# A decoder kernel: three places for the exponentials, squares moved right behind the maxima, and queries normed within the first step

## The chip, the cores and the metric

The kernel runs as one program on one core of a Trainium2 chip. The core has five engines with a queue of instructions each: PE multiplies matrices and transposes by a product with an identity matrix, DVE does elementwise work, reductions and transposes of 32x32 squares, ACT does activations and copies, POOL does elementwise work, and SP does nothing here but issue transfers. The metric is the device time of one execution in microseconds (us). The kernel before takes 907.77 us, the median of three runs (907.56 to 908.26).

## The reference

Eight sequences of 128 tokens with 512 features pass through two decoder layers. Each layer has an attention, a cross attention and a feed-forward block, each followed by a residual sum and a layer norm:

```python
x = _layernorm(x + _L0_attn_ref(x, ...))                 # causal, 32 heads of 16
x = _layernorm(x + _L0_xattn_ref(x, ctx_4096, ctx_4096)) # autocorrelation
x = _layernorm(x + _L0_ffn_ref(x, ...))                  # 28 experts of rank 8, two chosen
x = _layernorm(x + _L1_attn_ref(x, ...))                 # the block of the change
x = _layernorm(x + _L1_xattn_ref(x, ctx_4096, ...))      # 16 heads of 96, 4 key heads
x = _layernorm(x + _L1_ffn_ref(x, ...))                  # 8 adapters of rank 16
```

The change touches the second layer's causal attention alone:

```python
qkv = jnp.clip(jnp.einsum('bsd,ed->bse', hidden_states, Wqkv), -8.0, 8.0)
q, k, v = jnp.split(qkv, [512, 1024], axis=-1)
q = _layer_norm(q, q_ln_w, q_ln_b)       # mean and variance over all 512 features
k = _layer_norm(k, k_ln_w, k_ln_b)
# q, k, v are cut into 32 heads of 16
scores = jnp.einsum('bqhd,bkhd->bhqk', q, k) * 16 ** -0.5
scores = scores + slopes[None, :, None, None] * rel[None, None]   # distance of the tokens
scores = jnp.where(causal[None, None], scores, -1e30)
probs = jax.nn.softmax(scores, axis=-1)
out = jnp.einsum('bhqk,bkhd->bqhd', probs, v).reshape(B, S, 512)
return jnp.einsum('bsd,ed->bse', out, Wout)
```

## The kernel before

All in all the kernel goes through the six blocks one after the other, all in float32. The second causal attention occupies 335 to 533 us of the profiled execution. Before it lies the first layer, whose last experts still run at its beginning; behind it lie the second layer's cross attention and its feed-forward block. Some of the cross attention's projections (`front`) are drawn forward into the end of the causal attention.

**The loop.** Lines 974 to 1031 run over the eight sequences, b from 0 to 7; one b is called a *round* here. A round has two *steps*, f = 0 (the first step) and f = 2 (the second), each for 16 of the 32 heads. One step goes through these stages, most of them in the classes `Heads16` (line 164) and `Squares16` (line 315); every step is a `Squares16` but the last, (7, 2), which is a `Heads16`.

1. PE multiplies the queries qT with the keys kbd into the scores s_a, 32 small matmuls (line 184). The later 64 tokens are scored against all 128 keys, the earlier 64 against the first 64.
2. DVE adds the bias, writes the sum, negated, into the tile e and leaves the row's extreme value in m, one instruction for a head of both halves (line 222); this is called a *scoring*, there are 16 a step, 8 and 8. Between the two eights of the second step the moments of the next round's keys are put (`between`).
3. ACT takes the exponentials in place in e, and the row sums (line 235, `exps`).
4. `move` (line 336) turns the probabilities so that the keys lie on the partitions. DVE takes the reciprocals of the row sums (line 339), POOL copies them, spread out, into the last rows of e (line 340), and DVE transposes e within 32x32 squares in two instructions, the large one for the probabilities and the small one for the reciprocals (line 345). What is left is a permutation of whole squares, for which e goes through DRAM: one store of 896 KB into a tile `kept` (line 347) and four loads of 224 KB each into a tile pT (line 352), all issued by SP.
5. `out` multiplies pT with the values into o_a on PE (lines 291 and 297) and then calls `divided`, in which DVE multiplies with the turned reciprocals out of o_a's PSUM bank into oT (line 366).
6. `projection` (line 818) multiplies oT of a whole round with the output weights into po on PE, in two halves (line 823); DVE adds the residual (line 826), and the layer norm of that row follows later (`late_norms`, line 831).

**Steps overlap.** A step calls `move` of the step before it (`prev`), and `out` of three steps before it (`pending`). `projection` in the second step of round b is that of round b - 2. Beside this, each round prepares the next one's inputs: in the first step the products for the queries q and the keys k (`Normed`, line 763), in the second those for the values v and the turned tokens xT of the round after (PE, line 147). `Normed` multiplies on PE, and its `moments` clips q or k out of PSUM and takes mean and variance on DVE (lines 773 and 91 to 95), POOL raises the variance to the power -1/2 (line 97), and `norm` applies both on DVE (line 778) and, for k alone, the weights on POOL (lines 780 and 781). Then q and k are turned by PE (lines 801 and 812) and copied by ACT into qT (line 803) and kbd (line 815).

**What sets the order.** Under `in_order` (line 116) PE, DVE and ACT follow the program's order in this loop. For POOL and SP the scheduler decides the order. Waits come from the tiles: each tag has a number of places (`bufs`), given in turn, and who writes a place waits until the reader of its former content is done. In the loop, e and pT have two places each; q, k and xT have the pool `qp`'s number, qT and kbd the two of the pool `ap`, `kept` three in DRAM. PSUM has four single banks for o_a, po, the products of q, k and v and all turned tiles together (`bank`), and two double banks for the scores (`banks`).

In the kernel before, DVE's order in a first step, as lines 994 to 1008 set it, is: scorings; oT of `out`; moments of the late row; reciprocal, both transposes; the late row's norm; clip and moments of q. In a second step it is: norm of q; eight scorings; clip and moments of k; eight scorings; norm of k; oT of `out`; reciprocal, both transposes; clip of v; residual sum.

Of the kernel before, what the change touches and what calls it, by code (L numbers as in the profile page):

```python
# [11 lines left out]
F32 = mybir.dt.float32  # L12
# [5 lines left out]
P = 128  # L18
B, S, D = 8, 128, 512
NC = D // P  # L20
# [23 lines left out]
def decoder(ctx: ExitStack, tc: tile.TileContext, a: dict, out: bass.AP):  # L44
# [12 lines left out]
    def bank(name):  # L57
        return ps1.tile([P, 512], F32, tag="ps1", name=name)
# [105 lines left out]
    class Heads16:  # L164
# [8 lines left out]

        W = 3 * P

        def __init__(self, pool, units, bias, o_dst, name, between=(), places=1):
            self.pool, self.units, self.o_dst, self.name, self.rc = pool, units, o_dst, name, None
            self.places = places
            s = [banks(f"s_{name}_{i}") for i in range(2)]
            for part, cols, keys in ((0, slice(0, 2 * P), P), (1, slice(2 * P, 3 * P), 64)):  # L180
                for r in range(4):
                    rows = slice(32 * r, 32 * r + 32)
                    for u, (qT, kbd, _, _) in enumerate(units):
                        nc.tensor.matmul(  # L184
                            s[r // 2][64 * u : 64 * u + 64, r % 2, cols],
                            lhsT=qT[rows, 64 - 64 * part : P - 64 * part], rhs=kbd[rows, :, :keys],
                            start=True, stop=True,
                        )
            self.begin()
            self.m = sm.tile([P, 2, 4, 2], F32, tag="m", name=f"m_{name}")  # L190
            for i in range(2):
                while i and between:
                    between.pop(0)()
                with tc.issue_after(self.scored.ins) if i else nullcontext():
                    for part in range(2):
                        for r in (2 * i, 2 * i + 1):
                            for x in range(2):
                                self.head(s[i][:, r % 2], bias, part, r, x)
# [5 lines left out]
            return t[:, : 4 * self.W].rearrange("p (r k) -> p r k", r=4), t[:, 4 * self.W :]  # L204

        def begin(self):
            self.e, self.behind = self.rows("e", 2)
            self.su = sm.tile([P, 2, 4, 2], F32, tag="su_a", name=f"su_{self.name}")

        def cols(self, part, x):  # L210
# [71 lines left out]
            return self.pT[:, r, t * P + 64 * u : t * P + 64 * u + 64]  # L282

        def out(self):
            o = bank(f"o_{self.name}")
            for u, (_, _, v, vd) in enumerate(self.units):
                v, vd = (t() if callable(t) else t for t in (v, vd))
                late = slice(u * P + 64, u * P + P)
                for x in range(2):
                    for r in range(4):  # L290
                        nc.tensor.matmul(
                            o[32 * r : 32 * r + 32, late],
                            lhsT=v[:, 48 * r + 16 * x : 48 * r + 16 * x + 32],
                            rhs=self.probabilities(r, x, u), start=(x == 0), stop=(x == 1),
                        )
                for r in range(4):
                    nc.tensor.matmul(
                        o[32 * r : 32 * r + 32, u * P : u * P + 64],
                        lhsT=vd[:, 32 * r : 32 * r + 32],
                        rhs=self.probabilities(r, 2, u), start=True, stop=True,  # L300
                    )
            self.divided(o)

        def divided(self, o):
            if self.rc is not None:
                nc.vector.tensor_copy(self.o_dst, o[:, : 2 * P].rearrange("p (u q) -> p u q", u=2))
                return
            nc.vector.tensor_tensor(
                self.o_dst.rearrange("p u (a q) -> p u a q", a=2),
                o[:, : 2 * P].rearrange("p (u a q) -> p u a q", u=2, a=2),  # L310
                self.rT[:, ::-1].rearrange("p a (u q) -> p u a q", u=2),
                ALU.mult,
            )

    class Squares16(Heads16):
# [6 lines left out]


        def begin(self):
            self.tile = self.pool.tile([P, 4, 14, 32], F32, tag="e", name=f"e_{self.name}", bufs=2)
            self.e = self.tile[:, :, :12, :].rearrange("p g (r t) k -> p r t g k", r=4)
            self.sums = sm.tile([P, 4, 2, 2], F32, tag="su_a", name=f"su_{self.name}")
            self.su = self.sums.rearrange("p r a x -> p a r x")
# [31 lines left out]
        def probabilities(self, r, t, u):  # L360
            return self.pT[:, 2 * u : 2 * u + 2, 3 * r + t, :]

        def divided(self, o):
            by_half = "p u (a i q) -> p a u i q"
            rT = self.pT[:, :, 12:14, :].rearrange("p (u i) a q -> p a u i q", u=2)
            nc.vector.tensor_tensor(
                self.o_dst.rearrange(by_half, a=2, i=2),
                o[:, : 2 * P].rearrange("p (u t) -> p u t", u=2).rearrange(by_half, a=2, i=2),
                rT[:, ::-1],
                ALU.mult,  # L370
            )
# [391 lines left out]
    class Normed:  # L763

        def __init__(self, i, b, xT):
            self.i, n, w = i, *(("q", w1q), ("k", w1k))[i]
            self.name = f"{n}1_{b}"
            self.ps = bank(f"p{self.name}")
            mm_acc(self.ps, [(xT[:, c, :], w[:, c, :]) for c in range(NC)])
            self.rows = qp.tile([P, D], F32, tag=n, name=self.name)  # L770

        def moments(self):
            nc.vector.tensor_scalar(self.rows, self.ps, 8.0, -8.0, ALU.min, ALU.max)
# [21 lines left out]

    def turned_queries(b, q):
        q = q.rows
        qT = ap.tile([P, NC, P], F32, tag="qT", name=f"qT1_{b}")
        pt = bank(f"pTq1_{b}")
        for c in range(NC):  # L800
            nc.tensor.transpose(pt[:, c * P : (c + 1) * P], q[:, c * P : (c + 1) * P], ident)
        for c in range(NC):
            nc.scalar.activation(
                qT[:, c, :], pt[:, c * P : (c + 1) * P], AF.Identity, scale=lnq[:, 0, c : c + 1], bias=lnq[:, 1, c : c + 1]
            )
        return qT

    def turned_keys(b, k):
        k = k.rows
        pt = bank(f"pTk1_{b}")  # L810
        for c in range(NC):
            nc.tensor.transpose(pt[:, c * P : (c + 1) * P], k[:, c * P : (c + 1) * P], ident)
        kbd = ap.tile([P, 2, D], F32, tag="kbd", name=f"kbd1_{b}")
        for x in range(2):
            nc.scalar.mul(kbd[:, x, :], pt, pair[:, x : x + 1])  # L815
        return kbd
# [157 lines left out]
    for b in range(B):  # L974
# [4 lines left out]
        for f in (0, 2):  # L979
            units = []  # L980
            for i in (f, f + 1):
                feats = slice(i * P, (i + 1) * P)
                units.append((qT[:, i, :], kbd[:, :, feats], v_now[0][:, i * 192 : (i + 1) * 192], v_now[1][:, i * 128 : (i + 1) * 128]))
            if f and more:
                q.norm()
            kind = Heads16 if (b, f) == (B - 1, 2) else Squares16
            now = kind(
                ap, units, alibi_bias(f), oT[:, f : f + 2, :], f"a1_{b}_{f}", [k.moments] if f and more else [], places=2
            )
            now.exps(0)  # L990
            if f and more:
                k.norm()
            if len(pending) == 3:
                pending.pop(0).out()
            if f and more:
                qT = turned_queries(b + 1, q)
            now.divide(0)
            now.exps(1)
            now.divide(1)
            if f == 0:  # L1000
                if more:
                    q = Normed(0, b + 1, xT)
                normalize = late_norms()
                if prev:
                    prev.move()
                normalize()
                if more:
                    q.moments()
                if b == 0:
                    E7 = turned_gates(B - 1, routes[B - 1][1]), shared_expert(B - 1, *routes[B - 1])[1]  # L1010
                if more:
                    k = Normed(1, b + 1, xT)
                else:
                    front.go(2)
            else:
                prev.move()
                if more:
                    v = values(b + 1, xT)
                    if b + 2 < B:
                        xT = turned_tokens(b + 2)  # L1020
                else:
                    front.go(2)
                half = projection(b - 2, oTs.pop(b - 2)) if b > 1 else iter((0, 0))
                next(half)
                if b == 0:
                    chosen_experts(B - 1, *E7)
                if more:
                    qk = qT, turned_keys(b + 1, k)
                next(half)
            pending.append(now)  # L1030
            prev = now
# [507 lines left out]
```

## Time and profile before

| What | Value |
|---|---|
| median of three runs | 907.77 us (907.56 to 908.26) |
| the profiled execution, its own time | 910.55 us |
| span of the profiled execution | 908.7 us, mean granted clock of PE 0.975 |
| busy over the span | PE 848.1 us (93%), DVE 549.1 (60%), ACT 369.1 (41%), POOL 145.8 (16%) |
| busy from 335 to 533 us (198.0 us) | PE 162.1, DVE 133.5, ACT 111.2, POOL 43.3; granted clock 0.91 |
| stores and reloads of squares | 15 stores of 896 KB, median 4.5 us from issue to landing; 60 loads of 224 KB, 4.4 us |
| beginnings of the first scorings of rounds 1 to 7 | 354.20, 376.50, 398.77, 422.61, 447.26, 470.12, 495.15 us |

In the lines of the profile, L222 is line 222 of the kernel; `e_a<-s_a` names the tile written and the tiles read, where `_a` stands for this attention and the number of the buffer is left out. "x32" is the number of instructions in a group. In square brackets stands how long the engine was idle ahead of the group and, behind the arrow, what ended that. PE is the matmuls, PEld the loading of their weights beside them; the granted clock (PEclk) is the share of full speed at which the clock throttle let PE run.

### The profile page before, as it was taken

The numbers are of one execution on the slowest core, as the hardware profiler recorded it, in microseconds if no ns is written. First come the engines' busy times: TensorE is split into PE (matmuls) and PEld (weight loads), VectorE is DVE, ScalarE is ACT, GpSimd is POOL, SyncE is SP. The second block draws the span as 40 slices with busy tenths as digits, with TensorE's granted clock in tenths as the row PEclk, the third lists the DMA queues.
The fourth block names the chain that finished last, engine by engine and source line by source line (L and its number), as shares of the span: only waits on it lengthen the run. The fifth ranks groups of instructions, "written<-read, shape, count | busy, mean of one in ns | idle before, by whom it ended". The sixth has DMA issues, their size and how long they took to land.

```text
span 908.7 us, 17674 instructions
## 1 busy us (share of the span) xinstructions
PE 848.1 (93%) x6302; PEld 518.2 (57%) x6302; DVE 549.1 (60%) x2158; ACT 369.1 (41%) x1536; POOL 145.8 (16%) x224
## 2 busy tenths in 40 slices
PE   9999999999899998788897789999999999999996
PEld 5766656565345544344444458767566755677444
DVE  3656777886867647677776530654345544657654
ACT  3876665653232146666665301422212221224220
POOL 2400223233332302222222200000000000000001
PEclk9999999999999998899998989999999999999999
DMA  9700000122100015555458620132223222323340
GB/s 332 282 2 25 2 24 2 58 94 93 57 3 23 1 47 169 163 163 156 130 163 251 206 78 24 33 89 45 46 47 79 44 54 47 70 44 79 82 101 35
DMA packets 40872, 78.25 MB, mean 86 GB/s; under 512 B 6736, under 2 KB 30928, under 8 KB 38992
## 3 DMA queue, kind: packets, MB, share of 16 engines
q1 hardware_dynamic: 38224, 75.02, 27.8%
q10 hardware_dynamic: 2560, 2.10, 1.0%
q8 instruction: 50, 0.82, 0.4%
q14 instruction: 38, 0.31, 0.1%
HBM read 44.46 MB, written 15.86 MB: 66 GB/s over the span
## 4 chain that ended last, share of the span: by engine, by line
PE 60%; DVE 17%; DMA 8%; ACT 7%; POOL 3%; issue 2%; SPq 1%; ACTq 1%; POOLq 0%; DVEq 0%
PE pqx L86 9%; DMA kept_a<-e_a 6%; PE pox L1135 6%; DVE e_a L222 4%; ACT e_a L235 4%; PE pvx L86 4%; PE pq L86 4%; PE s_x L1073 4%; PE o_x L1118 4%; PE pkx L86 3%; PE pk L86 3%; PE pv L86 3%; PE pof L725 2%; PE s_a L184 2%; PE po L86 2%
## 5 line engine op out<-in xcount | busy, mean ns | idle before, releaser
L235 ACT ACTIVATE e_a<-e_a,m_a 128x128 f32<-128x128 f32 (+1 forms) x512 | 184.3, 364 | 112.1 <-DVE m_a L222 107.1
L1094 ACT ACTIVATE e_x<-s_x,m_x 128x256 f32<-128x256 f32 x128 | 58.6, 483 | 139.6 <-DVE m_x L1084 125.4
L235 ACT ACTIVATION_READ_ACCUMULATOR e_a<-e_a,m_a 128x1 f32 x512 | 97.1, 190 | 0.0
L86 PE MATMUL pqx<-xTx,w_X_q 128*128 128x256 f32 x384 | 84.9, 380 | 0.0
L86 PEld LDWEIGHTS pqx<-xTx,w_X_q 128*128 128x128 f32 x384 | 72.6, 190 | 11.4 <-issue 1.8
L1135 PE MATMUL pox<-w_X_o,oTx 128*128 128x512 f32 x168 | 74.1, 597 | 0.7 <-DVE oTx L1124 0.6
L222 DVE CUSTOM_DVE_ANT_0 e_a<-s_a,alibi 128x128 f32<-128x128 f32 (+1 forms) x256 | 47.5, 253 | 31.8 <-DMA kept_a<-e_a 25.3
L1083 DVE TENSOR_REDUCE m_x<-s_x 128x4 f32<-128x1024 f32 x32 | 37.6, 1219 | 41.6 <-PE s_x L1073 41.6
L1135 PEld LDWEIGHTS pox<-w_X_o,oTx 128*128 128x128 f32 x168 | 31.3, 190 | 40.9 <-issue 39.2
L1073 PE MATMUL s_x<-kTx,qTx 32*128 32x256 f32 x768 | 50.0, 385 | 0.7 <-ACT e_x L1094 0.7
L222 DVE CUSTOM_DVE_ANT_0 e_a<-s_a,masks 128x128 f32<-128x128 f32 (+1 forms) x256 | 47.2, 253 | 5.2 <-PE s_a L184 4.2
L1073 PEld LDWEIGHTS s_x<-kTx,qTx 32*128 32x128 f32 x768 | 39.0, 185 | 16.8 <-issue 11.7
L97 POOL TENSOR_TENSOR rs_x<-ve_x,neghalf 128x1 f32<-128x1 f32 x7 | 3.8, 548 | 268.6 <-DVE ve_x L95 249.6
L1118 PE MATMUL o_x<-pT_x,vx 128*32 128x512 f32 x384 | 43.7, 595 | 1.9 <-DMA pT_x<-e_x 1.2
L222 DVE DVE_READ_ACCUMULATOR2_ANT m_a<- 128x1 f32 x512 | 42.6, 83 | 0.0
L1102 DVE STREAM_TRANSPOSE e_x<-e_x 128x1024 f32<-128x1024 f32 x32 | 39.7, 1241 | 0.8
L964 ACT COPY qTx<-pqx 128x512 f32<-128x512 f32 x24 | 14.1, 593 | 63.4 <-PE pqx L86 63.4
L184 PEld LDWEIGHTS s_a<-kbd,qT 32*64 32x64 f32 x1024 | 22.0, 138 | 30.7 <-issue 18.0
L184 PE MATMUL s_a<-kbd,qT 32*64 32x256 f32 (+1 forms) x1024 | 35.0, 353 | 4.6 <-ACT kbd L815 2.7
L1101 DVE TENSOR_SCALAR e_x<-e_x,rc_x 128x256 f32<-128x256 f32 x128 | 36.3, 348 | 3.5 <-DVE rc_x L1098 2.0
L103 DVE TENSOR_TENSOR x_x<-pox,x_a 128x512 f32<-128x512 f32 x7 | 4.8, 686 | 52.5 <-PE pox L1135 52.5
L345 DVE STREAM_TRANSPOSE e_a<-e_a 128x1536 f32<-128x1536 f32 (+1 forms) x30 | 31.5, 1071 | 6.0 <-POOL e_a L340 6.0
(241 smaller groups left out, 1624.8 us busy)
## 6 DMA issues: line engine op xcount, KB each, us to landing
pT_x<-e_x SPq DMA_DIRECT2D x224, 64.0 KB, 2.0
kept_a<-e_a SPq DMA_DIRECT2D x15, 896.0 KB, 4.5
pT_a<-kept_a SPq DMA_DIRECT2D x60, 224.0 KB, 4.4
w_X_q<-in_X_q SPq DMA_DIRECT2D x3, 1024.0 KB, 6.2
w_X_o<-in_X_o SPq DMA_DIRECT2D x3, 1024.0 KB, 8.1
w_L_Wv<-in_L_Wv SPq DMA_DIRECT2D x2, 1024.0 KB, 7.3
w_L_Wo<-in_L_Wo SPq DMA_DIRECT2D x2, 1024.0 KB, 7.5
x_in<-in_x SPq DMA_DIRECT2D x8, 256.0 KB, 7.7
```

What stands on the lines that cost most here:

```text
L86: nc.tensor.matmul(ps, lhsT=l, rhs=r, start=(i == 0), stop=(i == n - 1))
L184: nc.tensor.matmul(s[r // 2][64 * u : 64 * u + 64, r % 2, cols], lhsT=qT[rows, 64 - 64 * part : P - 64 * part], rhs=kbd[rows, :, :keys], s ...
L222: self.scored = nc.vector.tensor_tensor_reduce(self.block(part, r, x), self.alike(s[:, cols]), self.alike(bias(r, cols)), -1.0, 3e38, ALU. ...
L235: nc.scalar.activation(e, e, AF.Exp, scale=-1.0, bias=self.m[:, part, r, x : x + 1], accum_out=self.su[:, part, r, x : x + 1],)
L345: nc.vector.transpose(self.tile[:, :, rows, :], self.tile[:, :, rows, :])
L1073: nc.tensor.matmul(sc[g // 2][:, g % 2, u * 256 : (u + 1) * 256], lhsT=qT[rows, (h0 + u) * NS + n, :], rhs=kT[rows, n], start=(n == 0), st ...
L1083: nc.vector.tensor_reduce(m, self.s[i], AX.X, ALU.max, negate=True)
L1094: nc.scalar.activation(self.e[:, :, j, :], self.s[half][:, i, :].rearrange("p (a k) -> p a k", k=32), AF.Exp, bias=self.m[:, j : j + 1], s ...
L1101: nc.vector.tensor_scalar(e, e, self.rc[:, j : j + 1], None, ALU.mult)
L1102: nc.vector.transpose(self.e[:, :, js, :], self.e[:, :, js, :])
L1118: nc.tensor.matmul(po[32 * g : 32 * g + 32, :], lhsT=v[:, s, g * XD + 32 * n : g * XD + 32 * n + 32], rhs=pT[:, s].rearrange("p i h x -> p ...
L1135: nc.tensor.matmul(po, lhsT=oT[:, n, h * P : (h + 1) * P], rhs=w, start=(i == 0), stop=(i == NX - 1))
```

## The change

The tile e gets three places in place of two, while pT keeps two (`places=(2, 3)`; the first number is pT's, the second e's). The tiles q, k, qT and kbd of this attention get one place each.

In both steps, `move` of the step before is called right behind the step's exponentials, so that DVE's reciprocal and transposes stand right behind the scorings and, in the second step, the norm of k. In the first step they were behind the late row's moments, in the second behind oT.

`out` is cut into `multiply` (the products on PE) and `divided` (oT on DVE). `multiply` stays where `out` was in PE's order; `divided` now comes behind `move` and, in the first step, behind the clip and moments of q as well.

In the first step, q's product and its moments come ahead of `divided` and the late row's moments, and the norm of q follows these, in the same step; before, the norm of q was the first thing of the second step.

Line numbers of the functions behind the cut grow by 4 to 8: the store L347 becomes L351, a load L352 becomes L356, the transposes L345 become L349, oT L366 becomes L371, k's operations L780 and L781 become L785 and L786, and po L823 becomes L828.

```diff
--- before.py
+++ after.py
@@ -173,9 +173,9 @@
 
         W = 3 * P
 
-        def __init__(self, pool, units, bias, o_dst, name, between=(), places=1):
+        def __init__(self, pool, units, bias, o_dst, name, between=(), places=(1, 2)):
             self.pool, self.units, self.o_dst, self.name, self.rc = pool, units, o_dst, name, None
-            self.places = places
+            self.places, self.room = places
             s = [banks(f"s_{name}_{i}") for i in range(2)]
             for part, cols, keys in ((0, slice(0, 2 * P), P), (1, slice(2 * P, 3 * P), 64)):
                 for r in range(4):
@@ -204,7 +204,7 @@
             return t[:, : 4 * self.W].rearrange("p (r k) -> p r k", r=4), t[:, 4 * self.W :]
 
         def begin(self):
-            self.e, self.behind = self.rows("e", 2)
+            self.e, self.behind = self.rows("e", self.room)
             self.su = sm.tile([P, 2, 4, 2], F32, tag="su_a", name=f"su_{self.name}")
 
         def cols(self, part, x):
@@ -282,7 +282,11 @@
             return self.pT[:, r, t * P + 64 * u : t * P + 64 * u + 64]
 
         def out(self):
-            o = bank(f"o_{self.name}")
+            self.multiply()
+            self.divided()
+
+        def multiply(self):
+            self.o = o = bank(f"o_{self.name}")
             for u, (_, _, v, vd) in enumerate(self.units):
                 v, vd = (t() if callable(t) else t for t in (v, vd))
                 late = slice(u * P + 64, u * P + P)
@@ -299,9 +303,9 @@
                         lhsT=vd[:, 32 * r : 32 * r + 32],
                         rhs=self.probabilities(r, 2, u), start=True, stop=True,
                     )
-            self.divided(o)
-
-        def divided(self, o):
+
+        def divided(self):
+            o = self.o
             if self.rc is not None:
                 nc.vector.tensor_copy(self.o_dst, o[:, : 2 * P].rearrange("p (u q) -> p u q", u=2))
                 return
@@ -322,7 +326,7 @@
 
 
         def begin(self):
-            self.tile = self.pool.tile([P, 4, 14, 32], F32, tag="e", name=f"e_{self.name}", bufs=2)
+            self.tile = self.pool.tile([P, 4, 14, 32], F32, tag="e", name=f"e_{self.name}", bufs=self.room)
             self.e = self.tile[:, :, :12, :].rearrange("p g (r t) k -> p r t g k", r=4)
             self.sums = sm.tile([P, 4, 2, 2], F32, tag="su_a", name=f"su_{self.name}")
             self.su = self.sums.rearrange("p r a x -> p a r x")
@@ -360,7 +364,8 @@
         def probabilities(self, r, t, u):
             return self.pT[:, 2 * u : 2 * u + 2, 3 * r + t, :]
 
-        def divided(self, o):
+        def divided(self):
+            o = self.o
             by_half = "p u (a i q) -> p a u i q"
             rT = self.pT[:, :, 12:14, :].rearrange("p (u i) a q -> p a u i q", u=2)
             nc.vector.tensor_tensor(
@@ -767,7 +772,7 @@
             self.name = f"{n}1_{b}"
             self.ps = bank(f"p{self.name}")
             mm_acc(self.ps, [(xT[:, c, :], w[:, c, :]) for c in range(NC)])
-            self.rows = qp.tile([P, D], F32, tag=n, name=self.name)
+            self.rows = qp.tile([P, D], F32, tag=n, name=self.name, bufs=1)
 
         def moments(self):
             nc.vector.tensor_scalar(self.rows, self.ps, 8.0, -8.0, ALU.min, ALU.max)
@@ -795,7 +800,7 @@
 
     def turned_queries(b, q):
         q = q.rows
-        qT = ap.tile([P, NC, P], F32, tag="qT", name=f"qT1_{b}")
+        qT = ap.tile([P, NC, P], F32, tag="qT", name=f"qT1_{b}", bufs=1)
         pt = bank(f"pTq1_{b}")
         for c in range(NC):
             nc.tensor.transpose(pt[:, c * P : (c + 1) * P], q[:, c * P : (c + 1) * P], ident)
@@ -810,7 +815,7 @@
         pt = bank(f"pTk1_{b}")
         for c in range(NC):
             nc.tensor.transpose(pt[:, c * P : (c + 1) * P], k[:, c * P : (c + 1) * P], ident)
-        kbd = ap.tile([P, 2, D], F32, tag="kbd", name=f"kbd1_{b}")
+        kbd = ap.tile([P, 2, D], F32, tag="kbd", name=f"kbd1_{b}", bufs=1)
         for x in range(2):
             nc.scalar.mul(kbd[:, x, :], pt, pair[:, x : x + 1])
         return kbd
@@ -981,31 +986,35 @@
             for i in (f, f + 1):
                 feats = slice(i * P, (i + 1) * P)
                 units.append((qT[:, i, :], kbd[:, :, feats], v_now[0][:, i * 192 : (i + 1) * 192], v_now[1][:, i * 128 : (i + 1) * 128]))
-            if f and more:
-                q.norm()
             kind = Heads16 if (b, f) == (B - 1, 2) else Squares16
             now = kind(
-                ap, units, alibi_bias(f), oT[:, f : f + 2, :], f"a1_{b}_{f}", [k.moments] if f and more else [], places=2
+                ap, units, alibi_bias(f), oT[:, f : f + 2, :], f"a1_{b}_{f}", [k.moments] if f and more else [], places=(2, 3)
             )
             now.exps(0)
             if f and more:
                 k.norm()
             if len(pending) == 3:
-                pending.pop(0).out()
+                older = pending.pop(0)
+                older.multiply()
+            else:
+                older = None
             if f and more:
                 qT = turned_queries(b + 1, q)
             now.divide(0)
             now.exps(1)
             now.divide(1)
+            if prev:
+                prev.move()
+            if f == 0 and more:
+                q = Normed(0, b + 1, xT)
+                q.moments()
+            if older:
+                older.divided()
             if f == 0:
+                normalize = late_norms()
                 if more:
-                    q = Normed(0, b + 1, xT)
-                normalize = late_norms()
-                if prev:
-                    prev.move()
+                    q.norm()
                 normalize()
-                if more:
-                    q.moments()
                 if b == 0:
                     E7 = turned_gates(B - 1, routes[B - 1][1]), shared_expert(B - 1, *routes[B - 1])[1]
                 if more:
@@ -1013,7 +1022,6 @@
                 else:
                     front.go(2)
             else:
-                prev.move()
                 if more:
                     v = values(b + 1, xT)
                     if b + 2 < B:
```

## The prediction, made before the changed kernel was run

> **What bounds the kernel now.** The page puts 93% of the span on PE, but the slices from 350 to 520 us, the second causal attention, are where the granted clock dips and PE, DVE and ACT are all partly idle. So I read that stretch alone, first its waits (engine and line, what it waited for, us in total, times, longest).
>
> ```profile
> ACT e_a L235 <- DVE m_a L222: 63.2, 15, 6.2
> ...
> DVE e_a L222 <- DMA kept_a<-e_a: 25.3, 12, 4.5
> ...
> PE pTk L812 <- POOL k L781: 13.6, 7, 5.1
> ...
> PE pTq L801 <- DVE q L778: 8.9, 5, 2.9
> ```
>
> The second row is the one at the end of the chain: the scorings of a step (L222) write an exponentials tile e, and with two places for e they must wait until the square store of two steps earlier (kept) has landed. ACT's 63.2 us only follow from it. Next the busy times by round (one b), a round running from the first scoring of its first step to that of the next.
>
> ```profile
> core 0: us, PE busy (x) PEld busy (x) DVE busy (x) ACT busy (x) POOL busy (x), PEclk, DMA share, GB/s
> ...
> 398.77:422.61 23.84, 20.33 (x208) 10.08 (x207) 17.79 (x88) 14.79 (x71) 5.66 (x9) 1.00 0.51 155
> 422.61:447.26 24.65, 19.87 (x203) 9.84 (x202) 17.79 (x89) 14.79 (x71) 5.66 (x9) 0.93 0.50 151
> 447.26:470.12 22.86, 20.64 (x205) 10.40 (x204) 17.86 (x89) 14.79 (x71) 5.66 (x9) 0.93 0.55 163
> 470.12:495.15 25.03, 19.86 (x159) 9.28 (x161) 17.79 (x88) 14.33 (x70) 5.65 (x9) 0.86 0.71 214
> ```
>
> PE needs some 20 us of a round's 24, DVE 17.8: little room above the store wait. Then DVE's and PE's order of time in the second step of round 3.
>
> ```profile
> 408.92 0.29 DVE L222 CUSTOM_DVE_ANT_0 e_a<-s_a,alibi 128x128 f32<-128x128 f32 x1 [0.38 <-DMA kept_a<-e_a]
> ...
> 413.50 0.54 DVE L778 TENSOR_SCALAR k<-k,mv_k,rs_k 128x512 f32<-128x512 f32 x1
> 413.96 0.42 DVE L366 TENSOR_TENSOR oT<-o_a,pT_a 128x256 f32<-128x256 f32 x1
> ...
> 414.46 1.72 DVE L345 STREAM_TRANSPOSE e_a<-e_a 128x1536 f32<-128x1536 f32 x1
> 417.11 0.45 DVE L345 STREAM_TRANSPOSE e_a<-e_a 128x256 f32<-128x256 f32 x1 [0.94 <-POOL e_a L340]
> ...
> 422.61 0.29 DVE L222 CUSTOM_DVE_ANT_0 e_a<-s_a,alibi 128x128 f32<-128x128 f32 x1 [2.72 <-DMA kept_a<-e_a]
> ```
>
> ```profile
> 412.59 0.60 PE L147 MATMUL pt_xTa<-ident,x_f 128*128 128x128 f32 x4
> 413.81 1.98 PE L823 MATMUL po<-w_L_Wo,oT 128*128 128x512 f32 x4 [0.62 <-ACT qT L803]
> 416.79 0.65 PE L812 MATMUL pTk<-ident,k 128*128 128x128 f32 x4 [1.00 <-POOL k L781]
> 417.28 1.88 PE L823 MATMUL po<-w_L_Wo,oT 128*128 128x512 f32 x4
> 419.10 0.91 PE L184 MATMUL s_a<-kbd,qT 32*64 32x256 f32 x32
> ```
>
> The next scores are there at 419.97, DVE starts on them at 422.61: 2.64 us of store wait. Last the granted clock around an idle PE (PEclk is the figure before the DMA share).
>
> ```profile
> 430.14:433.55 3.41, 1.03 (x6) 0.82 (x7) 1.50 (x4) 0.00 (x0) 0.55 (x1) 1.00 0.57 235
> 433.55:436.96 3.41, 3.41 (x6) 1.35 (x5) 2.25 (x18) 1.81 (x10) 0.00 (x0) 0.50 0.40 107
> ```
>
> PE stood still for 2.97 us (429.55 to 432.52), and the next 3.41 us ran at half clock.
>
> **The change part by part.**
> *Three places for e, one for q, k, qT and kbd.* In the built program a scoring now waits for the store of three steps earlier, landed some 10 us before. The wait is gone. What is late next is the score product s_a, that is PE. The single places cost nothing: each old reader (turning of q and k, score products) stands ahead of the new writer on PE, and its result has been awaited already.
>
> *Squares behind the maxima, first step.* On DVE from the first scoring: 16 scorings 2.85 (447.26 to 450.11), reciprocal 0.16, both transposes 1.96 (451.61 to 453.57), q's clip and moments 1.83 (453.99 to 455.82), oT 0.33, moments of the late row 1.09, q's norm 0.46, the row's norm 0.42: 9.1 us. q's norm no longer waits 0.67 for POOL, since oT and the moments lie between; the late row's own POOL power is now waited for, 0.67 less q's norm, 0.2. With hand-overs 9.4. Before: 10.15, 12.07, 10.19, 11.08 in rounds 3 to 6. PE beside it: o_a 0.81, pq 3.54, pk 3.53, s_a 0.84, 8.7, hidden by DVE's 9.4; at half clock that cover is gone.
>
> *Squares behind the maxima, second step.* Here the edit has a price. oT (L366) now follows the reciprocal and both transposes: 4.58 to k's norm, 0.46, 0.16, 1.65, 0.37, 0.42 and a hand-over of 0.06, 7.7 us after the first scoring instead of 5.5. In the built program the projection's first half (po) of rounds 3, 4 and 5 takes the PSUM bank that oT reads and waits for it; before, that bank was freed by ACT's qT. Queued behind po on PE: pTk, the other half, s_a. So 7.7 + 1.82 + 0.49 + 1.82 + 0.84 = 12.7 to the next scoring. Without the store wait the old order would give 11.05 (408.92 to 419.97); the new order costs 1.65 and the wait gives 2.64 back. In round 2 po still waits for qT, in round 6 for k's clip, and only pTk stands behind oT; it waits for POOL until 8.05 anyway: 8.05 + 0.49 + 1.82 + 0.84 + 0.05 = 11.25.
>
> *POOL.* The copy L340 now goes between the two operations on k (L780, L781). That ends the small transpose's 0.94 us wait and puts k off from 2.62 to 2.84 us (round 0 has this order), hidden behind po.
>
> *PE's new stand-still.* In rounds 3 to 5 PE is done with pt_xTa 4.5 us after the scoring began (s_a 0.7 ahead of it, o_a 0.81, pTq 0.47, pv 3.44, turn 0.43) and waits until 7.7: 3.2 us. The waits for q's norm (8.9 us) go in exchange. In the trace the clock changes only at marks 3.41 us apart; it fell after stand-stills of 2.97, 3.26 and once 1.9, held after two of 1.9, and stayed at half for 3.41 or 6.83. A stand-still of 3.2 misses a fall only if the marks cut it into pieces under 1.9, in (1.9 - 1.3)/3.41, 2 in 10. One window at half costs 1.7. Bounds 0 and 3.4 a round; I take 0.8 x 1.7 = 1.4, nearest to the 2.97 row, and 0.5 for round 6, which stands still only for 2.
>
> [...]
>
> *SP's queue.* Two loads are passed by a store: the reload pT of step (0,2) goes behind the store of (1,0), that of (6,2) behind the store of (7,0). The first then lands about 375 (store at 368.4, four issues of 1.73, landing 4.4), and PE's o_a in round 2 waits some 2 us for it. The second makes the last round's end longer: o_a of (6,2) comes 15.2 after the last scoring's start instead of 8.1, then, at a cold clock, po and the turn, 0.9 us net; bounds -1 and 3.5. The 1 MB load of X_o and the 528 KB of F1 move behind; first use 611, eighty us later.
>
> **The sum**, against the profiled execution (span 908.7, its own time 910.55, 2.8 above the median of 907.77).
> - Rounds 0 to 2: the scoring of round 1 starts at 351.3 with s_a instead of 354.20; round 1 is then bound by PE at the clock before shows; the late reload takes half back. Round 3 starts at 396.9 instead of 398.77: 1.9 saved, bounds 0 and 3.3.
> - Rounds 3 to 5: 71.35 before, 3 x (9.4 + 12.7 + 1.4) = 70.5: 0.85.
> - Round 6: 25.03 less 9.4 + 11.25 + 0.5: 3.9.
> - Round 7, first step: 11.74, less 4.46 of store wait, plus 0.67 for the late row's power: 3.8.
> - End: -0.9.
>
> Together 9.55 us. Behind it PE is the chain to the end, so the gain is kept: span 899.15, its own time 901.0, median 898.2.
>
> **The rivals.**
> - *The clock holds.* Nothing of the 4.7 us is lost: 14.25 saved, 893.5. For it: two stand-stills of 1.9 without a fall. Against: every one over 2 had one.
> - *The new wait eats it.* Two windows at half in each of rounds 3 to 6: 3.4 each, 8.9 more than forecast, 907.1. For it: 488.16 to 494.99 and 372.1 to 378.9 were at half for two windows, with PE waiting.
> - *Slower.* PE's clock, now on the path. Half-clock time between 351 and 524 was 27.6 us before, most of it under the store wait. In the changed kernel half of each such microsecond is lost at the end. The gain at full clock is 14.25, so from 28.5 us at half clock the kernel is slower; with two windows in each of six rounds, 41 us, it is 20.5 - 14.25 = 6.2 slower, 914.0. Against: dense first steps bring the clock back.
> - *It doesn't do what it says* (a scoring still waits for a store): the built program's waits exclude it, and a store would have to take 15 us instead of 3.6 to 5.5.
>
> **How the numbers follow.** About 0.2% (1.8 us) can be told from no change. Forecast 898.2, with 895 to 903 as its own range, 0.45. Clock holds 0.18. Between forecast and "eats it", near 904.5, 0.14. Eats it, 0.07, counted as same. Slower 0.16. Faster is 0.45 + 0.18 + 0.14 = 0.77. The range from 893 to 908 leaves out the slower case and little else.
>
> **What would show it.** Right: no row of DVE L222 waiting for kept; PE's po waiting some 3 us for oT in rounds 3 to 5 and hardly in rounds 2 and 6, with half clock behind it; pTq's wait gone; rounds 3 to 5 near 23.5, round 6 near 21; o_a of (0,2) and (6,2) waiting for their reload. Wrong: a full clock there, rounds of 25 us, or a stretch behind 533 that isn't simply shifted.

## The result, and the profile after

The changed kernel takes 910.97 us (median of six runs, 910.23 to 912.00), the kernel before 907.45 us in the same comparison: a ratio of 1.0043, with an interval from 1.0030 to 1.0056. It is 3.5 us slower, where 9.55 us less was forecast.

The profiled execution of the changed kernel has 910.77 us and a span of 908.9 us, that of before 910.55 and 908.7. The two traces look equally long because the one of before caught an execution 3.1 us above its median. A second profile of the kernel before, taken later (run `e7_before_again` below), has 906.56 and 904.7.

The waits of the changed kernel from 335 to 533 us, the second causal attention (engine and line, what it waited for, us in total, times, longest):

```profile
PE o_a L295 <- DMA pT_a<-kept_a: 13.7, 2, 9.4
...
DVE e_a L222 <- PE s_a L184: 11.8, 5, 4.4
...
PE po L828 <- DVE oT L371: 10.1, 3, 3.4
...
PE pTk L817 <- POOL k L786: 7.5, 3, 2.9
```

The row in which scorings waited 25.3 us for the stores is gone, and so is that of pTq for q's norm. Scorings now wait only for their scores, so PE sets the end, as forecast. But PE waits itself: 10.1 us for oT, as forecast, and 13.7 us in two places for reloads. These two are in PE's order of time here, the first in round 2, the second at the end:

```profile
376.46 0.66 PE L295 MATMUL o_a<-pT_a,v 128*32 128x64 f32 x16 [4.38 <-DMA pT_a<-kept_a]
...
521.09 0.66 PE L295 MATMUL o_a<-pT_a,v 128*32 128x64 f32 x16 [9.36 <-DMA pT_a<-kept_a]
```

SP's queue shows why. The row of 12.52 us holds two stores: those of (0,2) and of (1,0). The second waits for its transposes, and the reload of (0,2), long possible, stands behind it, so that eight loads leave within 5.4 us, the first four of them those of (0,2):

```profile
352.39 1.75 SPq L356 DMA_DIRECT2D pT_a<-kept_a  x4
355.05 12.52 SPq L351 DMA_DIRECT2D kept_a<-e_a  x2
368.05 5.34 SPq L356 DMA_DIRECT2D pT_a<-kept_a  x8
```

The end looks the same, with the stores of (6,2) and (7,0) in the first row:

```profile
499.89 12.29 SPq L351 DMA_DIRECT2D kept_a<-e_a  x2
512.27 6.12 SPq L356 DMA_DIRECT2D pT_a<-kept_a  x8
```

The busy times by round, rounds 3 to 5 (PE, PEld, DVE, ACT, POOL, then the granted clock, the DMA share, GB/s):

```profile
398.98:424.11 25.13, 21.78 (x212) 11.01 (x215) 17.79 (x89) 14.80 (x71) 5.90 (x9) 0.86 0.62 176
424.11:448.10 23.99, 20.64 (x212) 10.53 (x214) 17.78 (x88) 14.80 (x71) 5.90 (x9) 0.93 0.49 149
448.10:472.10 24.00, 20.65 (x212) 10.54 (x215) 17.79 (x89) 14.80 (x71) 5.91 (x9) 0.93 0.52 154
```

They were to take 23.5 and take 24.4 in the mean. The stretches, from the starts of the first scorings in each trace, in us (the end runs from the first scoring of step (7,2) to the end of the span; half clock is counted from 335 to 533 us):

| Stretch | before | before, second profile | after | forecast for after, against the first |
|---|---|---|---|---|
| up to the scoring of (0,2) | 339.52 | 338.36 | 338.06 | no change |
| (0,2) to round 2 | 36.98 | 35.92 | 34.06 | |
| round 2 | 22.28 | 22.32 | 26.87 | with the row above -1.9 |
| rounds 3 to 5 | 71.34 | 71.62 | 73.11 | -0.85 |
| round 6 | 25.04 | 24.42 | 22.67 | -3.9 |
| first step of round 7 | 11.74 | 11.11 | 7.96 | -3.8 |
| the end | 401.77 | 400.92 | 406.16 | +0.9 |
| half clock | 37.5 | 20.5 | 47.8 | |

### The profile page after: what moved, and what is told of

The parts are those of the page before. It is cut to its first block, busy times and chain, and to the rows that moved or that the text cites. A ratio compares the mean times of both kernels' runs of the same rounds, so it can differ in the third digit from the quotient of the medians.

```text
span 908.9 us, 17674 instructions
## 1 busy us (share of the span) xinstructions
PE 846.5 (93%) x6302; PEld 517.1 (57%) x6302; DVE 548.1 (60%) x2158; ACT 369.2 (41%) x1536; POOL 147.3 (16%) x224
## 4 chain that ended last, share of the span: by engine, by line
PE 68%; DVE 15%; ACT 7%; DMA 4%; issue 2%; POOL 2%; ACTq 1%; SPq 1%; POOLq 0%; DVEq 0%
PE pqx L86 9%; PE pq L86 6%; PE pox L1143 6%; PE pk L86 5%; ACT e_a L235 4%; PE s_x L1081 4%; PE pkx L86 4%; PE o_x L1126 4%; PE pvx L86 3%; PE po L828 3%; PE pv L86 3%; PE s_a L184 3%; DVE e_a L222 3%; PE pof L730 2%; DMA pT_a<-kept_a 2%; PE po L86 2%
## 5 line engine op out<-in xcount | busy, mean ns | idle before, releaser
L828 PE MATMUL po<-w_L_Wo,oT 128*128 128x512 f32 x64 | 37.8, 728 | 10.1 <-DVE oT L371 10.1
L295 PE MATMUL o_a<-pT_a,v 128*32 128x64 f32 x1024 | 25.6, 228 | 14.8 <-DMA pT_a<-kept_a 13.7
L184 PEld LDWEIGHTS s_a<-kbd,qT 32*64 32x64 f32 x1024 | 21.4, 136 | 30.7 <-issue 18.6
```

Of the source, the lines that this page charges most:

```text
L184: nc.tensor.matmul(s[r // 2][64 * u : 64 * u + 64, r % 2, cols], lhsT=qT[rows, 64 - 64 * part : P - 64 * part], rhs=kbd[rows, :, :keys], s ...
L828: nc.tensor.matmul(po, lhsT=oT[:, c, :], rhs=w1o[:, c, :], start=(c == 0), stop=(c == NC - 1))
```

## The experiments

Three theories stood against each other on the loss, that is, on what lies between the forecast and the result; a fourth, D, comes with its run. A: the two late reloads are most of it. B: PE's stand-still ahead of po is most of it. C: whatever is no longer waited for comes back as half-clock windows, so that no repair helps. Of each kernel the diff is to the changed kernel, unless another is named.

**The reloads back in front.** Each store is now ordered behind the previous step's reload.

```diff
-            nc.sync.dma_start(kept, self.tile.rearrange("p g r k -> p g (r k)"))
+            with tc.issue_after(Squares16.loaded.ins) if Squares16.loaded else nullcontext():
+                nc.sync.dma_start(kept, self.tile.rearrange("p g r k -> p g (r k)"))
...
             for g in range(4):
-                nc.sync.dma_start(to[32 * g : 32 * g + 32], by_group[:, :, g, :])
+                Squares16.loaded = nc.sync.dma_start(to[32 * g : 32 * g + 32], by_group[:, :, g, :])
```

> The changed kernel with one thing undone: on SP's queue each reload pT stands ahead of the next store again, as in the kernel before; all other queues are the same. Theory A (the two late reloads are most of the loss): in the changed kernel PE waited 4.4 us for the reload of (0,2) and 9.4 us for that of (6,2), round 2 took 26.9 us with 13.7 us of half clock around it, and 406.2 us lay behind the last scoring's start instead of 401.8. Without them round 2 should take 9.6 + 13.1 = 22.7 and the end 401.8, together 8.6 us less: 902.4. Theory B (the stand-still before po is most of the loss, the late reloads are hidden behind it or behind the clock): less than 3 us, 908 or more. Theory C (whatever is no longer waited for is lost again in half-clock windows): 909 to 911, with as much half-clock time as in the changed kernel (48 us from 346 to 525).

Measured: 900.15 us (899.72 to 901.72), ratio to before 0.9924 (0.9911 to 0.9936): 10.8 us less than the changed kernel, where theory A expected 8.6, and out of reach of B and C. SP's queue of this kernel, in the same place as above:

```profile
354.45 0.34 SPq L354 DMA_DIRECT2D kept_a<-e_a  x1
360.52 1.99 SPq L359 DMA_DIRECT2D pT_a<-kept_a  x4
366.87 0.34 SPq L354 DMA_DIRECT2D kept_a<-e_a  x1
370.44 1.74 SPq L359 DMA_DIRECT2D pT_a<-kept_a  x4
```

The reload of (0,2) leaves 7.5 us earlier. Round 2 takes 22.57 instead of 26.87, the end 403.04 instead of 406.16, and half clock falls from 47.8 to 30.7 us. One thing moved besides: po of round 2 now waits for oT too, since the banks fell differently; its second step takes 12.74 instead of 11.53, which hides 1.2 us of the gain. Rounds 3 to 5 still take 71.87, and each of their second steps 14.4.

**Only the reload at the end late.** As above, but the reload of (6,2) is issued right behind the store of (7,0), so that it alone stands where the changed kernel has it.

```diff
+            if Squares16.later:
+                Squares16.later.pop()()
...
+            def reload():
+                for g in range(4):
+                    Squares16.loaded = nc.sync.dma_start(to[32 * g : 32 * g + 32], by_group[:, :, g, :])
+            if self.name in ('a1_6_2',):
+                Squares16.later.append(reload)
+            else:
+                reload()
```

> The changed kernel with the reload of (0,2) ahead of the store of (1,0) again, while that of (6,2) stays behind the store of (7,0). It divides the 10.8 us that the two late reloads cost together (910.97 less 900.15). By the two traces, the end behind the last scoring's start took 406.2 us with it and 403.0 without: if that is the price of this one, 900.2 + 3.1 = 903.3, and the other one, whose round 2 was followed by four half-clock windows, costs the remaining 7.7. If the end is what counts and round 2's wait was taken from other waits: 907 or more.

Measured: 904.02 us (902.17 to 906.84, twelve runs), 0.9967 (0.9952 to 0.9981). So the late reload at the end costs 3.9 us, and the one in round 2 the other 7.0. The traces of the changed kernel and of this one are 7.9 us apart: 4.4 in round 2 itself and 0.7 ahead of it, and behind it 1.3 in rounds 3 to 5 and 1.7 in round 6, where in the changed kernel one half-clock window more falls into round 3 and into round 6 than in this one.

**Three places and nothing moved.** The kernel before, with the numbers of places changed alone.

```diff
-... tag="e", name=f"e_{self.name}", bufs=2)
+... tag="e", name=f"e_{self.name}", bufs=3)
-            self.rows = qp.tile([P, D], F32, tag=n, name=self.name)
+            self.rows = qp.tile([P, D], F32, tag=n, name=self.name, bufs=1)
... (qT and kbd with bufs=1 in the same way)
```

> The kernel before with three places for e and one for q, k, qT and kbd, and nothing moved. If a third place removes the store waits (25.3 us in 12) and what is late next is PE, rounds 3 to 5 should take 10.15 + 11.05 = 21.2 instead of 23.8, rounds 1, 2 and 6 some 2 us less each, and (7,2) should come 4 us earlier: 18 us less at full clock, of which I expect a quarter to be lost to half-clock windows: 894. Theory C expects 904 or more.

Measured: 887.80 us (886.12 to 890.34), 0.9786 (0.9769 to 0.9803): 19.4 us faster than before, more than expected. In rounds 3 to 5 first steps take 9.68 and second steps 11.19, and between 373.9 and 472.9 us there is no half-clock window at all. The places alone are thus a gain of 2.1%; what the single places of q, k, qT and kbd do in it was not measured apart. Theory C falls here. On SP the reloads stand ahead of the next store, as in the kernel before. And po already waits for oT, four times and 2.6 us in all: the bank that oT frees comes with the places.

**The moves with two places.**

```diff
-... [k.moments] if f and more else [], places=(2, 3)
+... [k.moments] if f and more else [], places=(2, 2)
```

> The changed kernel with two places for e, so only the moves. SP's order is then that of the kernel before, and po waits for ACT's qT and not for oT. Scorings wait for the store of two steps earlier again, but that is issued sooner: transposes done 5 us after the first scoring in a first step, 7.4 in a second, and the store 4.5 us later: first steps 9.6 to 10, second steps 12.2, rounds 3 to 5 about 22 instead of 23.8. Theory A: the moves alone are a gain, 897 to 900, and the third place brought the late reloads and the wait for oT. If the moves themselves are what costs (theory D, DVE's new order), it is 910 or more.

Measured: 895.69 us (894.15 to 897.79), 0.9872 (0.9856 to 0.9888). The moves alone are a gain of 11.5 us: stores are issued sooner, and scorings wait for them 8.0 us in all instead of 25.3. DVE's order is that of the changed kernel, but po waits for qT, and rounds 3 to 5 have second steps of 11.5 to 11.6, store waits included, against 14.4 in the first experiment. So it is not DVE's new order by itself that makes them long (theory D). Each half of the change is a gain. Put together, they have two things that neither half has. Two reloads go behind a store; in both halves SP keeps each reload ahead of the next store, as in the kernel before, and why the scheduler turned it for the two together is not shown. And po waits for a late oT: the places bring the bank, the moves the lateness.

**oT ahead of the squares in the second step.** Reloads in front, as in the first experiment, and:

```diff
+            if f and older:
+                older.divided()
             if prev:
                 prev.move()
...
-            if older:
+            if f == 0 and older:
                 older.divided()
```

> As the run before, and in the second step oT stands ahead of the reciprocal and the transposes again; the first step keeps the new order and e its three places. Theory A says that both prices are gone: po waits for an oT that comes 5.5 us after the first scoring instead of 7.7 to 8.2, second steps fall from 14.4 to 11.1 (before's 11.05 without the store wait), rounds 3 to 5 to 20.7 plus at most 0.8 of half clock, some 3 us less each; rounds 2 and 6 about 1 us less: 902.4 - 9 - 2 = 891. Theory B: the same drop of about 11 us, from 908: 897. Theory C: PE falls to half clock in other places, 905 or more.

Measured: 887.08 us (885.73 to 889.86), 0.9783 (0.9764 to 0.9803): 13.1 us less than the first experiment. Rounds 3 to 5 at full clock (same columns as above):

```profile
392.35:413.11 20.76, 19.17 (x212) 9.64 (x215) 17.79 (x89) 14.79 (x71) 5.94 (x9) 1.00 0.58 177
413.11:433.87 20.76, 19.24 (x212) 9.68 (x214) 17.80 (x89) 14.80 (x71) 5.93 (x9) 1.00 0.62 180
433.87:454.62 20.75, 19.16 (x212) 9.64 (x214) 17.79 (x88) 14.80 (x71) 5.94 (x9) 1.00 0.60 179
```

Beside the third experiment (887.80) nothing is left of the moves: with three places and both orders kept, what the first step's new order saves (9.57 for 9.68) is no longer to be told from no change.

**Both reloads late, on the old order.** The kernel before with three places (887.80), and the reloads of (0,2) and (6,2) behind the next store, by the means of the second experiment.

> The kernel before with three places (887.8), and both reloads put behind the next store as in the changed kernel; none of the moves on DVE. If the late reloads are a price of SP's order by itself, they cost here what they cost there, 7.7 and 3.1, or somewhat less where the clock falls less: 895 to 899, 898 by the sum. If they only hurt together with the new order on DVE: 888 to 890.

Measured: 900.10 us (897.73 to 902.00), 0.9920 (0.9898 to 0.9941). The two late reloads cost 12.3 us here, more than there and more than expected. Round 2 takes 27.14 instead of 21.06 and the end 405.56 instead of 401.23. It is SP's order by itself that costs.

**The kernel before again.**

> The kernel before a second time, for a second profile, since the one at hand is of an execution 3 us above the median. The rounds of the second causal attention should be those of the first profile (rounds 3 to 5 about 23.8 each, 25 us of waiting for the stores), and the 3 us in half-clock windows or ahead of 329 us.

Measured: 906.56 us, span 904.7. Rounds 3 to 5 take 71.62 (71.34 in the first profile), the scorings wait for stores 26.2 us. It reaches (0,2) 1.2 us sooner than the first profile; the stretch behind is 2.8 us shorter, and has 20.5 us of half clock instead of 37.5.

**Idle products in the stand-still.** The first experiment's kernel, with products that nobody reads on PE ahead of the turning of the tokens, in the second steps of rounds 2 to 5; the turned tokens overwrite them.

```diff
+        def filler(pt):
+            for _ in range(2 if b > 3 else 0):
+                nc.tensor.matmul(pt, lhsT=ident, rhs=w1o[:, 0, :], start=True, stop=True)
```

> The same with two idle products. Here po of rounds 2 to 5 waits for oT as in the first run, and PE stands still for 2.4 us instead of 3.4. Stand-stills of 2.97 and more were followed by a half-clock window in the trace of before, two of 1.9 were not. If the clock holds: second steps of 12.8, 900.15 - 4 x 1.6 = 893.8. If it falls: 14.4 and 900.

Measured: 894.46 us (894.31 to 896.14), 0.9865 (0.9842 to 0.9887): 5.7 us faster with more work on PE. In rounds 3 to 5 the clock holds (1.00 in each), and the second steps take 12.74. Round 6, which has no idle products, gets a half-clock window that the first experiment does not have there (22.6 us for 21.0). PE's order of time in round 3 (the first row holds the idle products; each takes 0.86 us, since it counts as two in the trace):

```profile
407.94 1.88 PE L773 MATMUL pt_xTa<-w_L_Wo,ident 128*128 128x512 f32 x4
409.65 0.60 PE L149 MATMUL pt_xTa<-ident,x_f 128*128 128x128 f32 x4
411.90 1.98 PE L838 MATMUL po<-w_L_Wo,oT 128*128 128x512 f32 x4 [1.65 <-DVE oT L376]
413.72 0.60 PE L827 MATMUL pTk<-ident,k 128*128 128x128 f32 x4
```

PE still waits for oT, 1.65 us instead of 3.35, and po starts where it did, 7.7 us after the first scoring (404.18). All that is gone is the half clock behind it, 1.63 us a step.

**Five idle products.**

> The first run's kernel (the moves, three places, reloads first; 900.15), with five idle products of 128x512 on PE (0.46 us each) ahead of the turning of the tokens in the second steps of rounds 2 to 5; they write into the bank that the turned tokens overwrite. The program's banks fall differently: po of rounds 3 and 5 takes the bank that qT frees, po of rounds 2 and 4 that of oT. Round 4 keeps the wait for oT but PE stands still for 1.1 us instead of 3.4. If the 14.4 us of its second step are 12.7 of waiting and 1.7 of half clock brought on by the stand-still, it takes 12.8 at full clock; if they are the wait and the order alone, 14.4. In rounds 3 and 5 the wait for oT is gone although DVE's order is the new one: 11.7 if the bank is what costs, 14 or more if the order on DVE costs. Time in the first case 900.15 - 1.6 - 2 x 2.7 = 893.

Measured: 899.59 us (897.99 to 900.65), 0.9920 (0.9898 to 0.9942). It tells nothing on the bank. The expectation took 0.46 us for a product, from a row that counts each twice; five take 4.3 us, so that PE is busy until after oT in rounds 2 to 5, po waits for nothing, and each second step of rounds 3 to 5 takes 13.4. It shows only that the clock holds in rounds 3 to 5 here too (pv takes 3.60 us in rounds 3 and 4, as in the run with two products, whose granted clock is 1.00).

**Norms spread over DVE.** The kernel of 887.08, with k's moments ahead of the second step's scorings, its norm between the eights, and the late row's norm in the second step.

```diff
+            if f and more:
+                k.moments()
...
-... [k.moments] if f and more else [], ...
+... [k.norm] if f and more else [], ...
...
-                normalize()
+                if not more:
+                    normalize()
...
                     if b + 2 < B:
                         xT = turned_tokens(b + 2)
+                    normalize()
```

> The second run's kernel (three places, reloads first, oT first; 887.08) with two more moves on DVE. The moments of k go ahead of the second step's first eight scorings and its norm between the eights, so that k leaves POOL about 6.3 us after the first scoring instead of 7.7 and PE's wait for it (1.25 us a round) goes; and the late row's norm goes from the first step, which DVE bounds at 9.57, to the second. First steps 9.57 - 0.42 - 0.2 = 8.95, second steps 10.85 (PE's own work) instead of 11.18: 0.95 a round in six rounds, 881. Rival: DVE's second step gets too full or the scorings come late for ACT, and it stays at 887.

Measured: 887.04 us (884.81 to 888.97), 0.9777 (0.9753 to 0.9800): nothing gained. The wait of pTk for k is nearly gone (0.5 us in all instead of 8.8), but the second step's s_a then waits for ACT's kbd, 4.1 us in three rounds, and a round takes 20.69 instead of 20.76. The three fastest kernels of the study thus can't be told apart: 887.04, 887.08, and the simplest, 887.80, which is the kernel before with the places changed.

## Why the prediction was wrong

Right, by its own steps: the store wait goes, and with it pTq's wait; PE sets the end. First steps were to take 9.4 and take 9.58. The wait of po for oT exists in rounds 3, 4 and 5 and in no other, 3.35 us long (3.2 was forecast). The second step without half clock was put at 12.7: the run with two idle products measured 12.74. The first step of round 7 gained 3.78, for 3.8 forecast.

Wrong in three terms. Between the forecast, 9.55 us less, and the result, 3.5 us more, lie 13.1 us; by the stretches of the two traces the first two terms make up 11.2 of them.

- *SP's queue.* This is the step that failed. It was seen that the reload of (0,2) goes behind the store of (1,0) and that of (6,2) behind the store of (7,0), but they were priced at some 2 us in round 2, half of the saving there, and 0.9 net at the end. They cost 7.0 and 3.9. In the sum the two stood at about 2.3 us (1.4 of the 3.3 of rounds 0 to 2, and 0.9), and the first experiment measured 10.8: this term alone is some 8.5 of the 13.1 us. In round 2 the landing was put at about 375 and came at 376.4, and PE waited 4.38; the clock was at half already, and stayed there for four windows instead of the two that it has with the reloads in front. At the end o_a was put 15.2 us behind the last scoring's start and came 18.4 behind it: the store of (7,0) and eight reloads were under way together, and these reloads took 5.2 to 7.1 us to land instead of the median of 4.4. The stated bound of 3.5 for the end was passed by the 4.4 of the two traces. By stretches, the time from the scoring of (0,2) to round 3 gained nothing but lost 1.7 (forecast 1.9 gained), and the end lost 4.4 (forecast 0.9).
- *The clock behind PE's stand-still.* It was given 8 chances in 10 a round at 1.7. The price was right (1.63), the chances were not independent: in the changed kernel half clock begins at 442.49, 466.38 and 490.27 us, 23.89 apart, which is seven of the marks (7 x 3.413), and a round of 24.0 us is nearly as long. So the marks stay nearly where they are within the round, and the clock fell in every one of rounds 3 to 5, with two windows in round 3 (from 415.18). In the first experiment the granted clock is 0.93 in each of the three rounds, which is one window at half a round. Rounds 3 to 5 took 73.1 for 70.5 forecast. Round 6 took 22.7 for 21.15; there a window fell too. Without the late reloads it took 20.98. So of the 4.1 us by which rounds 3 to 6 exceed the forecast, the second experiment gives 3.0 to the late reload of round 2; with the reloads in front rounds 3 to 5 take 71.87, 1.4 over the forecast, 0.5 of it in the first steps. By itself the clock's term was short by about 1 us.
- *The base.* The savings were taken from a trace with 37.5 us of half clock and set against the median; the second profile of before has 20.5. The remaining 1.9 us of the gap would be of this kind: behind (0,2) the second profile is 2.8 us shorter than the first. One reading in the prediction is slightly off: between 351 and 524 us the first profile has 27.9 us of half clock, not 27.6.

The rival *Slower* had the right sign and about the right size: it put 914.0 at 41 us of half clock between 351 and 524, and 43 us there gave 911. But it looked for them in two windows in each of six rounds; in the trace 24 of the 43 lie around the two late reloads, of which 13.7 are there with the reloads in front too. *The clock holds* put 893.5, without the 4.7 us (3 x 1.4 + 0.5) that the sum has for half clock; with the reloads in front and the two idle products, 894.46 was measured. That is near it, but not its case: from 335 to 533 us 23.9 us of half clock are left there. *It doesn't do what it says* is out: no scoring waited for a store.

Theory B was not the whole but a large part: the wait for oT, its half clock and what follows cost 13.1 us between the first experiment and the one with oT first. It takes two things together. In DVE's new order with po in another bank (two places) second steps take 11.5 to 11.6; in the bank of oT with oT early they take 11.2 (three places alone, or oT first); in that bank with oT late they take 14.4. The waits of po in the first experiment, in the one with oT first and in the one with two places, from 374 to 475 us, where po waits for oT, for oT and for qT:

```profile
PE po L831 <- DVE oT L374: 12.6, 4, 3.4
...
PE po L831 <- DVE oT L374: 3.6, 4, 1.1
...
PE po L828 <- ACT qT L808: 1.6, 3, 0.6
```

No run changed po's bank in the kernel with three places and left all else, so the first of these rests on the kernel with two places.

## What to carry to other kernels

Where a scheduler orders a queue, a change of buffers can reorder transfers that it never mentions: read each queue's order in the built program, and price a load that falls behind a store by the wait that the store itself makes in the queue, with all loads then leaving at once (here 12.52 us for the row of the two stores, then eight loads within 5.4). Here the change of places alone was worth 19.4 us and the moves alone 11.5, and together, with two late reloads and a bank that a late oT frees, they lost 3.5; so try the halves of a change apart. And the half clock that was seen behind a gap on PE belongs to the gap's price: here it was 1.63 us a step, and filling part of the gap with useless products was worth 5.7 us.

## What the runs showed of the hardware

In the traces of the kernel before and of the changed one the granted clock changes at marks 3.413 us apart: half clock begins in the changed kernel at 415.18, 442.49, 466.38 and 490.27 us, eight, seven and seven of them apart. The length of a stand-still alone does not tell there whether half clock follows. In the kernel before, PE stood still for 1.89 us up to 408.69 and for 1.90 us up to 457.17, each time in a window in which it was busy for 1.52 us; the next window was at full clock the first time and at half the second. It stood still for 2.05 us up to 232.68, with the mark at 232.15 in between, was busy for 1.89 and 2.89 us in the two windows, and the clock held; so the prediction's "every one over 2 had one" is true of the second causal attention, not of the whole trace. From 345.65 it stood still for 1.96 us, all in one window with 1.45 us of work, and the next window ran at half. Here is the window in which PE stood still in round 4 of the changed kernel, and the one that followed (the figure before the DMA share is the granted clock):

```profile
439.08:442.49 3.41, 1.09 (x3) 0.62 (x4) 2.86 (x4) 2.76 (x15) 3.13 (x5) 1.00 0.18 78
442.49:445.90 3.41, 3.41 (x9) 1.76 (x8) 0.00 (x0) 0.80 (x2) 0.36 (x1) 0.50 0.59 203
```

PE was busy for 1.09 of 3.41 us, and the next window ran at half. These are single readings of two traces; what sets the clock was not shown.

A late transfer cost more than its wait here. In round 2 of the changed kernel PE waited 4.38 us for the reload while the clock was at half already: in the windows from 367.39, 370.80 and 374.22 us it was busy for 1.42, 1.28 and 1.17 us, each was followed by another at half, and full clock came back at 381.05, after a window in which PE was busy throughout. The late reload in round 2 cost 7.0 us in all, by the second experiment.
